# A list scheduler inside a kernel and its model of transfers: one path that all transfers pass in a line at one rate

## The chip, the cores and the metric

The kernel runs on one core of a Trainium2 chip. A core has five engines that run side by side, each with its own queue of instructions that it works off in order: TensorE (PE in the profile, with its weight loads as PEld), VectorE (DVE), ScalarE (ACT), GpSimd (POOL) and SyncE (SP). Transfers between the memories run on 16 DMA engines; here SP issues the plain ones and POOL the accumulating ones. The metric is the device time of one execution in microseconds (us); smaller is better.

## The reference

The input `x` is 32 images of 96 channels of 56 x 56 numbers. There are two layers. The first is an inverted-bottleneck convolution; the second works on the 3136 pixels of an image as tokens, mixes them by a Fourier transform, and ends with a two-layer network that rounds to 8-bit and 16-bit floats.

```python
# layer 0 (biases and batch norms are folded into the weights here)
h = relu(bn(einsum('oc,bchw->bohw', w1, x)))      # 96 -> 576 channels
h = relu(bn(dwconv3x3(h, wdw)))                   # 9 taps for each channel
x = x + bn(einsum('oc,bchw->bohw', w2, h))        # 576 -> 96
# layer 1, on tokens t of shape (32, 3136, 96)
h = relu(bn(layernorm(t) @ w1.T))                 # 96 -> 192
X = fft(h, axis=1)
xr = relu(X.real * rd - X.imag * id + rb)
xi = relu(X.imag * rd + X.real * id + ib)
t = t + bn(ifft(xr + 1j * xi).real @ w2.T)        # 192 -> 96
u = q8(layernorm(t))                              # rounded to e5m2
h = relu(q16(q16(u @ q8(W1).T) + q8(b1)))         # 96 -> 384
t = t + q16(q16(q8(h) @ q8(W2).T) + q8(b2))       # 384 -> 96
```

## The kernel before

The kernel cuts the work into some hundred *steps* for each image: a load, a group of matmuls, an eviction, one tap of the convolution, and so on. Each step names its engine, its estimated cost, the steps that it comes after, the buffers that it takes and gives back, and a rank. When the program is built, `Plan.emit` plays all steps through on a clock of its own: whenever an engine of the model is idle, it emits the ready step of the lowest rank whose buffers are free. **The order in which the steps are emitted is the order of the instructions in each engine's queue on the chip.** The clock of the model is never seen by the chip; the chip waits on semaphores, as the data demand. So a wrong estimate makes no wrong result, only an order in which an engine may stand before data that are not there yet.

```python
class Plan:
    LATE = {"PE": 0.3, "ACT": 0.18, "DVE": 0.15}   # from a step's end to those that wait for it
    ...
    def emit(self):
        ...
                    s.emit()                       # the real instructions are issued here, in this order
                    left -= 1
                    idle[engine] = False
                    cost = self.stretched(now, s.cost) if engine == "PE" else s.cost
                    ...
                    late = self.moved(now, s.late) if isinstance(s.late, tuple) else s.late
                    heapq.heappush(events, (now + cost, count, engine, None))   # the engine is free again
                    heapq.heappush(events, (now + cost + late, count + 1, None, s))  # followers may start
        ...
                if engine == "PE" and idle[engine] and work and now > FIRST and self.sparse(now):
                    self.filler()                  # a matmul that nobody reads, where TensorE would pause
```

A step that issues a transfer has a tuple as its `late`: the bytes, a rate and a fixed extra time. `moved` makes of it the time until the transfer's landing:

```python
    def moved(self, now, moves):
        size, rate, extra = moves
        start = now + 1.4
        end = start + size / rate
        self.moving = [m for m in self.moving if m[1] > start - 20]
        wait = sum(max(0.0, min(end, b) - max(start, a)) for a, b in self.moving)
        self.moving.append((start, start + 1.3 * size / rate))
        return end + wait + extra - now
...
    def read(n):
        return n * 4, 170e3, 1.5       # bytes, bytes per us, us
    def written(n):
        return n * 4, 170e3, 3.0
```

The convolution of layer 0 is where most transfers with an impatient reader lie. A *unit* is 128 channels of half an image, eight of them for an image. ScalarE makes the first tap and one or two further products, VectorE adds the other taps one by one, and an accumulating transfer of GpSimd adds the product to the sum; then ScalarE applies the relu in place, and TensorE reads the sum:

```python
        def add(to, dr):                           # line 678: acc += product, or product += product
            def f():
                ...
                nc.gpsimd.dma_start(out=..., in_=..., accum_op=ALU.add)
        def finish():                              # line 687
            nc.scalar.activation(acc[img, s, k], acc[img, s, k], AF.Relu)

        t = step("ACT", act(W, 2, 0.09), begin, e, ["acc"], rank=4 * n + OFF[1])        # line 643
        c = [step("ACT", act(W, 1, 0.09), product(0), e, ["product"], rank=4 * n + AT[0])]  # line 659
        ...
        for at, q in enumerate(rest):              # line 670, on DVE
            t = step("DVE", dve(W - 28, 0.16), tap(*q), [t] + c * last, [], ["hs"] * last, rank=...)
        if k in DOUBLE:                            # two units of four: product += product first
            c = [step("POOL", 1.0, add(0, -up), c, [], ["product"],
                      late=(W * 128 * 4, 200e3, 0.0), rank=4 * n + AT[1])]
        t = step("POOL", 1.0, add(None, 0), [t] + c, [], ["product"],
                 late=(W * 128 * 4, 200e3, 0.0), rank=4 * n + 3)
        ready[img, s, k] = step("ACT", act(W, 0, 0.09), finish, [t], rank=4 * n + OFF[3])
```

Other transfers: `xs` (half an image of input, 623,616 bytes), `tdr` (layer 0's result to memory, 602,112), `ydr` (first transform stage to memory, 602,112 in four pieces), `yb` (the same back in another order, 602,112 in two pieces), `wb` (702,464) and `wd` (357,504) with transform constants, `gdr` and `gd` (301,056 each, out and back), `tt` (301,056) and the output (301,056). Line 837 is the square root of a norm on ScalarE, line 853 the reciprocal on VectorE behind it; line 1491 is the filler.

Of the kernel before, what the change touches and what calls it, by code (L numbers as in the profile page):

```python
# [52 lines left out]
W = R * S  # L53
# [75 lines left out]
PACE = {"last": 3.023, "front": 0.4, "mid": 0.54, "back": 0.45}  # L129
CHAIN = 0.6  # L130

SPARSE = 0.75
FILLER = 0.23
FIRST = 15.0
# [2 lines left out]
AT = (3.0, 0.5)  # L137
# [6 lines left out]
class Step:  # L144
    def __init__(self, engine, cost, emit, after, take, give, late, rank, at):
        self.engine, self.cost, self.emit = engine, cost, emit
        self.take, self.give, self.late = take, give, late
        self.rank, self.at = rank, at
        self.left = len(after)
        self.next = []  # L150
        for a in after:
            a.next.append(self)


class Plan:
# [12 lines left out]
    def __init__(self, free):  # L168
        self.free = dict(free)
        self.steps = []  # L170
        self.now = self.pace = 0.0
        self.window, self.share, self.slow = 0, {}, False
        self.moving = []
        self.filler, self.recent = None, []

    def stretched(self, now, work):
# [18 lines left out]
    def sparse(self, now):  # L195

        self.recent = [r for r in self.recent if r[1] > now - self.WINDOW]
        return sum(b - max(a, now - self.WINDOW) for a, b in self.recent) < SPARSE * self.WINDOW

    def moved(self, now, moves):  # L200

        size, rate, extra = moves
        start = now + 1.4
        end = start + size / rate
        self.moving = [m for m in self.moving if m[1] > start - 20]
        wait = sum(max(0.0, min(end, b) - max(start, a)) for a, b in self.moving)
        self.moving.append((start, start + 1.3 * size / rate))
        return end + wait + extra - now

    def job(self, now, pace):  # L210

# [2 lines left out]
    def step(self, engine, cost, emit, after=(), take=(), give=(), late=None, rank=None):  # L214
        late = self.LATE.get(engine, 0.1) if late is None else late
        if rank is None:
            rank = self.now
            self.now += self.pace
        s = Step(engine, cost, emit, list(after), list(take), list(give), late, rank, len(self.steps))
        self.steps.append(s)  # L220
        return s
# [62 lines left out]
def tile_kernel(ctx: ExitStack, tc: tile.TileContext, d: dict, out: bass.AP):  # L284
# [12 lines left out]
    def psum():  # L297
        return psa.tile([128, 2, 512], F32, name="ps", tag="ps")
# [147 lines left out]
    for k in range(NK + 1):  # L446
# [5 lines left out]
            start=True,  # L452
# [101 lines left out]
    step = plan.step  # L554

    def pe(n, m, passes):
        return passes * max(0.855 * n, 0.88 * m) / 1000

    def act(n, columns=0, source=0.05):
        return source + 0.835 * n / 1000 + 0.093 * columns  # L560

    def dve(n, fixed=0.13):
        return fixed + n / 960

    def read(n):
        return n * 4, 170e3, 1.5

    def written(n):
        return n * 4, 170e3, 3.0

    bands_set = [step("DVE", 1.2, bands(j), rank=2.0 + j) for j in range(2)]
    sets = []
    for n, (f, count) in enumerate(((second, 7), (attention, 6), (mixer, 21), (ffn, 4))):
        t = step("SP", 0.55 * count, fetch, sets[-1:], late=(150e3, 170e3, 1.5), rank=-20.0 + n)
        sets.append(step("DVE", 3.0, f, sets[-1:] + [t], rank=14.0 + 4 * n))
    second_set, mixer_set, *mid_set = sets

# [22 lines left out]
    def unit(img, s, k):  # L600
        n = (2 * img + s) * NK + k
        o = R * s - base[s]
        up = 1 - 2 * s
        u = {}

        def weight(dr, dc):
            at = 3 * (dr + 1) + dc + 1
            return wdw[:, k, at : at + 1]

        def expand(h):  # L610
            def mm():
                if h == 0:
                    u["hs"] = w2.tile([128, XR, S], F32, name="hs", bufs=3)
                u[h] = psum()
                for j in range(2):
                    at = (2 * h + j) * QW
                    nc.tensor.matmul(  # L617
                        u[h][:, j, 0:QW],
                        lhsT=w1T[:, 128 * k : 128 * (k + 1)],
                        rhs=xs[img, s][0:C, at : at + QW],  # L620
                        start=True,
                        stop=True,
                    )

            def evict():
                flat = u["hs"].rearrange("p r c -> p (r c)")
                nc.scalar.activation(  # L627
                    flat[:, 2 * h * QW : 2 * (h + 1) * QW].rearrange("p (j w) -> p j w", j=2),
                    u[h][:, :, 0:QW],
                    AF.Relu,  # L630
                    bias=b1[:, k : k + 1],
                )

            after = [loaded[img, s]] if h == 0 else [u["first"]]
            e = u["first"] = step("PE", pe(QW, 128, 4), mm, after, ["ps"] + ["hs"] * (h == 0), rank=4 * n + OFF[0] + h)
            return step("ACT", act(2 * QW, 1), evict, [e], [], ["ps"], rank=4 * n + OFF[0] + h)

        e = [expand(0), expand(1)]

        def begin():  # L640

            acc[img, s, k] = w1.tile([128, R, S], F32, name="acc", bufs=7)
            nc.scalar.activation(  # L643
                acc[img, s, k],
                u["hs"][:, o + up : o + up + R, :],
                AF.Identity,
                scale=weight(up, 0),
                bias=bd[:, k : k + 1],
            )

        def span(dr, dc):

            return max(0, -(o + dr)), min(R, XR - o - dr), max(0, -dc), S - max(0, dc)

        def product(dr):
            def f():
                ra, rb, _, _ = span(dr, 0)
                u["p", dr] = w1.tile([128, R, S], F32, name="product", bufs=3)
                nc.scalar.activation(  # L659
                    u["p", dr][:, ra:rb, :], u["hs"][:, ra + o + dr : rb + o + dr, :], AF.Copy, scale=weight(dr, 0)  # L660
                )

            return f

        def tap(dr, dc):
            def f():
                ra, rb, ca, cb = span(dr, dc)
                src = u["hs"][:, ra + o + dr : rb + o + dr, ca + dc : cb + dc]
                dst = acc[img, s, k][:, ra:rb, ca:cb]
                nc.vector.scalar_tensor_tensor(dst, src, weight(dr, dc), dst, ALU.mult, ALU.add)  # L670

            return f

        def add(to, dr):
            def f():
                ra, rb, _, _ = span(dr, 0)
                t = acc[img, s, k] if to is None else u["p", to]
                nc.gpsimd.dma_start(  # L678
                    out=t[:, ra:rb, :].rearrange("p r c -> p (r c)"),
                    in_=u["p", dr][:, ra:rb, :].rearrange("p r c -> p (r c)"),  # L680
                    accum_op=ALU.add,
                )

            return f

        def finish():
            nc.scalar.activation(acc[img, s, k], acc[img, s, k], AF.Relu)  # L687

        t = step("ACT", act(W, 2, 0.09), begin, e, ["acc"], rank=4 * n + OFF[1])
        c = [step("ACT", act(W, 1, 0.09), product(0), e, ["product"], rank=4 * n + AT[0])]  # L690
        rest = [q for q in TAPS[1:] if q != (up, 0)]
        if k in DOUBLE:

            rest.remove((-up, 0))
            c.append(step("ACT", act(W, 1, 0.09), product(-up), e, ["product"], rank=4 * n + AT[1]))
        for at, q in enumerate(rest):
            last = q == rest[-1]
            t = step("DVE", dve(W - 28, 0.16), tap(*q), [t] + c * last, [], ["hs"] * last, rank=4 * n + OFF[2] + at * 3.5 / len(rest))
        if k in DOUBLE:
            c = [step("POOL", 1.0, add(0, -up), c, [], ["product"], late=(W * 128 * 4, 200e3, 0.0), rank=4 * n + AT[1])]  # L700
        t = step("POOL", 1.0, add(None, 0), [t] + c, [], ["product"], late=(W * 128 * 4, 200e3, 0.0), rank=4 * n + 3)
        ready[img, s, k] = step("ACT", act(W, 0, 0.09), finish, [t], rank=4 * n + OFF[3])

    def last_channels(img, s):
# [160 lines left out]
    def front(img, s):  # L865
# [80 lines left out]
        for i in range(G):  # L946
# [14 lines left out]
            if i in (3, 6):  # L961
                a = i - i % 4
                ev.append(step("ACT", act((i + 1 - a) * 2 * C), evict(a, i + 1), t, [], ["pw"]))
        taken[img, s] = t[0]
        sent[img, s] = step("SP", 0.1, keep, ev, late=written(2 * SK * G * C))
        t = norm(u, "a", RP, SK, ev, False, ["norma"], [])
        for j in range(2):
            mixer_in(img, s, j, u, t)

    def mixer_in(img, s, j, v, after):  # L970
# [87 lines left out]
        def send():  # L1058

            yv = ydr[img].rearrange("ri g (b p) h -> b (ri g) (p h)", b=2)  # L1060
            for b in range(2):
                for c in range(2):
# [4 lines left out]
                    )  # L1067

        sent[img, "y", h] = step("SP", 0.3, send, ends, [], ["ya"], late=written(SK * G * HA))


# [487 lines left out]
```

## Time and profile before

| what | value |
|---|---|
| time, median of 3 executions (lowest to highest) | 4589.91 us (4589.24 to 4595.37) |
| span of the profiled execution | 4584.2 us, 88412 instructions |
| TensorE clock granted, mean | 0.988 of full speed |
| accumulating transfers, GpSimd's queue | 304.64 MB, 34.4% of the DMA engines' time |
| plain transfers, SyncE's queue | 479.15 MB, 36.2% of the DMA engines' time |
| chain that ended last, by engine | PE 48%, ACT 22%, DVE 16%, DMA 8%, issue 4% |

The profile is one execution on the chip. A *group* is all instructions of one source line on one engine; of each the profile gives the busy time, the mean duration and the engine's idle time just before them, with what ended it. "ACT acc L687 <- DMA acc<-product" reads: ScalarE stood idle before instructions of line 687, which write `acc`, until a transfer from `product` to `acc` had landed. The busy share of an engine is taken over the whole span; in a full pipeline the idle time of the fullest engine is the most that another order can win.

### The profile page before, as it was taken

What the parts mean: (1) busy time and instruction counts of PE and PEld (TensorE: products, weight loads), DVE (VectorE), ACT (ScalarE), POOL (GpSimd) and SP (SyncE); (2) the same over time, 40 slices, a digit from 0 to 9 for tenths busy, and PEclk for the clock granted to TensorE, in tenths of its full rate; (3) what the DMA queues carried; (4) which work ended last, traced back from release to release, by engine and by line L of the source; (5) the groups of instructions that cost most, each with busy time, mean ns of one, the idle gap of its engine ahead of it and who ended that gap; (6) DMA issues with size and microseconds to landing.
All of it is one profiled execution on the core that took longest, in us unless ns stands there. A gap on an engine that the chain in (4) does not pass through costs nothing.

```text
span 4584.2 us, 88412 instructions
## 1 busy us (share of the span) xinstructions
PE 4405.4 (96%) x35128; PEld 3296.1 (72%) x35128; DVE 4330.6 (94%) x7053; ACT 4114.5 (90%) x5390; POOL 340.7 (7%) x403
## 2 busy tenths in 40 slices
PE   8989999999999999999999999999999999999998
PEld 5667776777777777777777777777777777777777
DVE  8998999999999999999999999999999999999967
ACT  5677999999999999999999999999999999999965
POOL 1000000000000000000000000000000000000000
PEclk9999999999999999999999999999999999999999
DMA  4666777767767777767777767777767777767663
GB/s 104 135 155 157 190 171 176 187 162 185 181 163 188 174 179 185 184 166 191 173 176 185 183 163 188 174 176 183 187 162 188 174 174 190 179 165 191 168 170 107
DMA packets 390993, 789.44 MB, mean 172 GB/s; under 512 B 135696, under 2 KB 236628, under 8 KB 390580
## 3 DMA queue, kind: packets, MB, share of 16 engines
q1 hardware_dynamic: 335028, 479.15, 36.2%
q0 software_dynamic: 55488, 304.64, 34.4%
q8 instruction: 276, 4.52, 0.4%
q14 instruction: 137, 1.12, 0.1%
q10 hardware_dynamic: 64, 0.01, 0.0%
HBM read 286.38 MB, written 192.68 MB: 105 GB/s over the span
## 4 chain that ended last, share of the span: by engine, by line
PE 48%; ACT 22%; DVE 16%; DMA 8%; issue 4%; POOLq 0%; ACTq 0%; POOL 0%; SPq 0%; DVEq 0%
PE pw L883 11%; DVE acc L670 10%; PE ps L617 9%; DMA acc<-product 7%; PE ps L1005 4%; PE ps L1123 4%; PE ps L755 3%; PE ps L1036 3%; ACT product L659 3%; ACT hs L627 2%; ACT acc L687 2%; ACT acc L643 2%; PE ps L1329 2%; ACT h L1410 2%; ACT h L1395 2%
## 5 line engine op out<-in xcount | busy, mean ns | idle before, releaser
L670 DVE SCALAR_TENSOR_TENSOR acc<-hs,wdw,acc 128x1540 f32<-128x1540 f32 (+2 forms) x1664 | 2970.3, 1792 | 26.6 <-ACT acc L643 20.8
L617 PE MATMUL ps<-xs,w1T 96*128 96x406 f32 x2048 | 819.8, 523 | 24.6 <-ACT h L1395 16.7
L883 PEld LDWEIGHTS pw<-w2T,acc 128*112 128x112 f32 x7168 | 754.3, 178 | 62.1 <-issue 36.4
L883 PE MATMUL pw<-w2T,acc 128*112 128x96 f32 x7168 | 790.8, 264 | 4.5 <-ACT acc L687 4.5
L659 ACT ACTIVATE product<-hs,wdw 128x1568 f32<-128x1568 f32 (+1 forms) x384 | 613.8, 1599 | 21.6 <-DMA product<-product 20.9
L617 PEld LDWEIGHTS ps<-xs,w1T 96*128 96x128 f32 x2048 | 368.2, 194 | 261.7 <-issue 174.0
L627 ACT ACTIVATE hs<-ps,b 128x812 f32<-128x812 f32 x512 | 481.5, 941 | 51.2 <-PE ps L617 46.8
L687 ACT ACTIVATE acc<-acc 128x1568 f32<-128x1568 f32 x256 | 387.5, 1514 | 90.9 <-DMA acc<-product 85.1
L678 POOL DMA_DIRECT2D acc<-product x256 | 222.7, 870 | 3193.9 <-DVE mf L859 781.6
L643 ACT ACTIVATE acc<-hs,bd,wdw 128x1568 f32<-128x1568 f32 x256 | 437.0, 1707 | 0.3
L755 PE MATMUL ps<-hl,band 128*64 128x385 f32 (+3 forms) x3072 | 416.1, 495 | 0.3 <-ACT hs L627 0.3
L1005 PE MATMUL ps<-watt,xnT 97*120 97x192 f32 x1792 | 345.3, 337 | 60.9 <-DVE V L1152 59.6
L1005 PEld LDWEIGHTS ps<-watt,xnT 97*120 97x120 f32 x1792 | 299.0, 187 | 125.3 <-DVE V L1152 65.6
L1123 PEld LDWEIGHTS ps<-wb,yb 112*128 112x128 f32 x3528 | 297.3, 164 | 66.5 <-issue 20.9
L1395 ACT ACTIVATE h<-ps 128x784 f16<-128x784 f32 x384 | 319.6, 835 | 25.8 <-PE ps L1383 22.0
L1350 ACT ACTIVATE u<-tt,mf,rf 112x96 fp8e5<-112x96 f32 x812 | 312.3, 460 | 16.6 <-DVE mf L859 16.5
L1123 PE MATMUL ps<-wb,yb 112*128 112x112 f32 x3528 | 321.8, 271 | 4.4 <-ACT hs L627 2.6
L1410 ACT ACTIVATE h<-h 128x784 fp8e5<-128x784 f16 x348 | 301.9, 867 | 14.9 <-DVE h L1401 14.8
L755 PEld LDWEIGHTS ps<-hl,band 128*64 128x64 f32 (+1 forms) x3072 | 151.9, 134 | 198.9 <-issue 164.2
L1152 DVE SCALAR_TENSOR_TENSOR sb<-ps,cw,V 128x784 f32<-128x784 f32 x192 | 197.0, 1026 | 31.1 <-ACT V L1136 25.4
L1018 ACT ACTIVATE z<-ps 120x768 f32<-120x768 f32 (+1 forms) x256 | 182.3, 725 | 44.9 <-PE ps L1005 44.9
L1036 PE MATMUL ps<-z,wa 56*64 56x384 f32 (+1 forms) x2048 | 217.5, 496 | 0.3
(171 smaller groups left out, 6663.3 us busy)
## 6 DMA issues: line engine op xcount, KB each, us to landing
acc<-product POOLq DMA_DIRECT2D x256, 784.0 KB, 8.0
product<-product POOLq DMA_DIRECT2D x128, 756.0 KB, 10.1
yb<-ydr SPq DMA_DIRECT2D x252, 294.0 KB
wd<-in_wd_dram SPq DMA_DIRECT2D x128, 349.1 KB
wb<-in_wb_dram SPq DMA_DIRECT2D x63, 686.0 KB
ydr<-ya SPq DMA_DIRECT2D x256, 168.0 KB
xs<-in_x_dram SPq DMA_DIRECT2D x64, 609.0 KB
tdr<-xt SPq DMA_DIRECT2D x64, 588.0 KB
```

The source lines that it names most:

```text
L617: nc.tensor.matmul(u[h][:, j, 0:QW], lhsT=w1T[:, 128 * k : 128 * (k + 1)], rhs=xs[img, s][0:C, at : at + QW], start=True, stop=True,)
L627: nc.scalar.activation(flat[:, 2 * h * QW : 2 * (h + 1) * QW].rearrange("p (j w) -> p j w", j=2), u[h][:, :, 0:QW], AF.Relu, bias=b1[:, k ...
L643: nc.scalar.activation(acc[img, s, k], u["hs"][:, o + up : o + up + R, :], AF.Identity, scale=weight(up, 0), bias=bd[:, k : k + 1],)
L659: nc.scalar.activation(u["p", dr][:, ra:rb, :], u["hs"][:, ra + o + dr : rb + o + dr, :], AF.Copy, scale=weight(dr, 0))
L670: nc.vector.scalar_tensor_tensor(dst, src, weight(dr, dc), dst, ALU.mult, ALU.add)
L687: nc.scalar.activation(acc[img, s, k], acc[img, s, k], AF.Relu)
L755: nc.tensor.matmul(pv[:, :, ca:cb], lhsT=band[rows, j, dc + 1, 64 * o : 64 * o + 64], rhs=H[rows, q : q + 7, ca + dc : cb + dc], skip_grou ...
L883: nc.tensor.matmul(u["pw"][0:SK, t, n % 4, 0:C], lhsT=src[rows, (G * t + n) * SK : (G * t + n + 1) * SK], rhs=rhs, skip_group_check=True, **k,
L1005: nc.tensor.matmul(pv[0:PK, q - a, 0:HA], lhsT=xnT[:, q, 0:PK], rhs=watt, start=True, stop=True,)
L1123: nc.tensor.matmul(o, lhsT=lhsT, rhs=u["wb"][:, G * s + q, :], start=True, stop=True)
L1395: nc.scalar.activation(u["h", c].rearrange("p (j w) -> p j w", j=2), u["H", c][:, :, 0:n], AF.Copy)
L1410: nc.scalar.activation(u["h8"][:, c, :], u["h", c], AF.Copy, saturate=False)
```

## The change

Only the scheduler's model of transfers changes. Before, every transfer had a rate of its kind (170 GB/s, or 200 GB/s for accumulations) and was lengthened by its overlap with the intervals of the others, each drawn out by 1.3; what those others had been lengthened by themselves was not counted. After, all transfers share one path: each starts on it when the one before has left it, and no sooner than 1.0 us after its issue; it passes at 225 GB/s, and lands 0.5 us after it has left the path, or 1.3 us after if it is one of GpSimd's accumulations. The purpose is an estimate that keeps account of a backlog, so that the order of the steps fits the time at which data really come. Costs, ranks, buffers and every emitted instruction's form are as before.

```diff
+RATE = 225e3
+HARD = 0.5
+SOFT = 1.3
...
-        self.moving = []
+        self.moving = 0.0
...
     def moved(self, now, moves):
 
-        size, rate, extra = moves
-        start = now + 1.4
-        end = start + size / rate
-        self.moving = [m for m in self.moving if m[1] > start - 20]
-        wait = sum(max(0.0, min(end, b) - max(start, a)) for a, b in self.moving)
-        self.moving.append((start, start + 1.3 * size / rate))
-        return end + wait + extra - now
+        size, extra = moves
+        self.moving = max(self.moving, now + 1.0) + size / RATE
+        return self.moving + extra - now
...
     def read(n):
-        return n * 4, 170e3, 1.5
+        return n * 4, HARD
 
     def written(n):
-        return n * 4, 170e3, 3.0
+        return n * 4, HARD
...
-        t = step("SP", 0.55 * count, fetch, sets[-1:], late=(150e3, 170e3, 1.5), rank=-20.0 + n)
+        t = step("SP", 0.55 * count, fetch, sets[-1:], late=(150e3, HARD), rank=-20.0 + n)
...
-            c = [step("POOL", 1.0, add(0, -up), c, [], ["product"], late=(W * 128 * 4, 200e3, 0.0), rank=4 * n + AT[1])]
-        t = step("POOL", 1.0, add(None, 0), [t] + c, [], ["product"], late=(W * 128 * 4, 200e3, 0.0), rank=4 * n + 3)
+            c = [step("POOL", 1.0, add(0, -up), c, [], ["product"], late=(W * 128 * 4, SOFT), rank=4 * n + AT[1])]
+        t = step("POOL", 1.0, add(None, 0), [t] + c, [], ["product"], late=(W * 128 * 4, SOFT), rank=4 * n + 3)
```

## The prediction

> **What bounds the kernel now.** I read the page's busy times first, then the waits of each engine, then three whole image periods, and last the instructions around the one wait on a transfer that recurs in every image.
>
> ```profile
> PE 4405.4 (96%) x35128; PEld 3296.1 (72%) x35128; DVE 4330.6 (94%) x7053; ACT 4114.5 (90%) x5390; POOL 340.7 (7%) x403
> ...
> DMA packets 390993, 789.44 MB, mean 172 GB/s; under 512 B 135696, under 2 KB 236628, under 8 KB 390580
> ...
> acc<-product POOLq DMA_DIRECT2D x256, 784.0 KB, 8.0
> product<-product POOLq DMA_DIRECT2D x128, 756.0 KB, 10.1
> ```
>
> Three engines are nearly full. VectorE (DVE) is the floor: its 4330.6 us cannot shrink, because the change adds and removes no instruction of it. TensorE's 4405.4 us contain 207.1 us of filler matmuls (the group of line 1491, 1382 of them), which only fill its pauses, so its own work is about 4198 us. The whole span leaves DVE idle for 4584.2 - 4330.6 = 254 us. The stretch from 4350 us to the end alone has 234 us with 83.95 + 48.46 + 35.24 = 168 us of DVE work, so 66 us of that idle time is the last image draining, and 23 us more lie in the first 230 us. Some 165 us remain in the 4120 us between, and only these can be won or enlarged by another order.
>
> The next view is of busy times in three image periods (start:end, length, then each engine's busy us with its count). An image's period is the distance between two equal points of its work.
>
> ```profile
> 1055.50:1195.50 140.00, 136.15 (x1078) 101.33 (x1076) 133.20 (x215) 130.11 (x174) 10.45 (x12) 0.98 0.72 176
> 1612.90:1749.70 136.80, 133.17 (x1078) 99.00 (x1076) 133.06 (x215) 129.80 (x174) 10.46 (x12) 1.00 0.74 181
> 2161.30:2299.00 137.70, 134.62 (x1078) 99.81 (x1076) 133.20 (x215) 130.18 (x174) 10.46 (x12) 0.99 0.74 178
> ```
>
> DVE (third busy figure) has 133.1 to 133.2 us in each; only its pauses differ: 6.8, 3.7 and 4.5 us. From the 530.3 us to the 4259.7 us mark are 27 such periods, 138.1 us on average.
>
> Who waits, from 1000 to 4350 us, in ACT's and DVE's own lists (total us, times, longest):
>
> ```profile
> ACT acc L687 <- DMA acc<-product: 48.6, 24, 3.2
> ACT al L784 <- PE ps L755: 32.4, 25, 1.3
> ...
> DVE rf L853 <- ACT sdf L837: 42.4, 47, 2.5
> DVE sb L1152 <- ACT V L1136: 19.9, 50, 0.4
> ```
>
> ACT's longest wait is on a transfer, the accumulation of a product, just once per image. No wait of TensorE names a transfer. Here is that wait in one image, in the timeline (start, us, engine, line; idle before it in brackets):
>
> ```profile
> 2154.31 0.28 SPq L1301 DMA_DIRECT2D wd<-in_wd_dram  x1
> ...
> 2155.40 0.86 POOL L678 DMA_DIRECT2D acc<-product  x1 [14.74 <-DVE da L834]
> ...
> 2156.51 0.86 POOL L678 DMA_DIRECT2D product<-product  x1 [0.25 <-ACT product L659]
> ...
> 2164.24 1.51 ACT L687 ACTIVATE acc<-acc 128x1568 f32<-128x1568 f32 x1 [1.22 <-DMA acc<-product]
> ...
> 2165.66 0.19 ACT L837 ACTIVATE sdf<-wf 112x7 f32<-112x7 f32 x1
> ...
> 2165.89 0.20 DVE L853 RECIPROCAL rf<-sdf 112x7 f32<-112x7 f32 x1 [0.55 <-ACT sdf L837]
> ```
>
> The scheduler put the relu (L687) on ACT's queue 1.22 us before its sum had landed; the square root (L837) stands behind it, and DVE's reciprocal waits 0.55 us for that. In the 140.0 us period the same three places show 1.99 us on ACT and 1.31 us on DVE. So one forecast error of the scheduler becomes idle time of the floor engine.
>
> **What the Trainium skill says.** "Perfetto Trace Analysis", section "Tensor Engine Instruction (MATMUL, LD_WEIGHTS)", states that ACT and DVE are strict FIFO; the timeline agrees: work behind the relu stands still with it. "DMA: Bandwidth & Descriptors", section "Issuing engines are not separate DMA queues", says transfers of all issuers run on the same 16 DMA engines and interleave. The trace agrees on the shared path: an accumulation takes between 5.6 and 17.4 us to land, whatever else moves. Its section "Queues, rings and completion order" says that each DMA engine goes round the queues packet by packet. So a later transfer can delay an earlier one of another queue, which a strict line denies. The trace agrees here too: the product accumulation issued at 2190.09 had nothing ahead of it but landed after 10.1 us, as three more transfers were issued in the next microsecond.
>
> **The change, part by part.** Its direct work on the chip is zero: same matmuls, vector operations and transfers. What differs is the list scheduler's guess of when a transfer lands, so where the steps that need it stand in the queues. The number of fillers may move too.
>
> The constants. A lone accumulation (802,816 B) was forecast at 1.4 + 802816/200000 = 5.41 us, and becomes 1.0 + 802816/225000 + 1.3 = 5.87; the shortest landing in the trace is 5.6. A lone 602,112 B load goes from 1.4 + 3.54 + 1.5 = 6.44 to 1.0 + 2.68 + 0.5 = 4.18, and a store of that size from 7.94 to 4.18. The rate is plausible: the four largest queues' shares (36.2, 34.4, 0.4, 0.1%) sum to 71.1% at a mean of 172 GB/s, thus 172/0.711 = 242 GB/s when all are busy.
>
> The line. Before, the waiting time was the overlap with others' undelayed intervals, so a backlog was forgotten. I put the real issue times up to 2156.51 through both formulas (the scheduler's own issue times differ somewhat). New: the line starts at 2136.16, 1.0 after a 702,464 B load. Issued by 2155.40 are that, 602,112, 802,816, two of 301,056, two of 602,112, 623,616, 602,112, 357,504 and the accumulation's 802,816 B: 6,299,776 B, or 28.0 us at 225 kB/us. It leaves the line at 2164.16 and lands at 2165.46, 10.1 us after issue. The trace has 8.8 us (2164.22). The product behind it: 2164.16 + 3.57 + 1.3 = 2169.03; the trace has 2168.7. Old: start 2156.80, end 2160.81; the only overlap is 1.64 us with the wd load's interval (2155.71 to 2158.44), hence 2162.45, 7.05 us: 1.8 us too early. The product's old forecast is 9.96 us against 12.2. So at the wait that recurs, the new forecast is late enough for other ready work, the L1410 and L627 steps that stood behind the relu, to go first.
>
> The same calculation for all accumulations between 300 and 4300 us gives these errors (trace less forecast): into acc, 232 of them, old mean 0.32 with a standard deviation of 1.56 us, new 0.22 with 0.95; between products, 116, old mean 2.56, new 1.32. The new model is better here. Loads get shorter forecasts, from 7.8 to 6.0 us on average; their truth I cannot see in these records.
>
> The worth. ACT's waits on both kinds of accumulation are 85.1 + 20.9 = 106 us in the whole run, but ACT is not the floor. What reaches DVE: of the 42.4 us of DVE's rf wait, about 0.41 us in each of 24 periods is another visit that no transfer causes (9.8 us); 32.6 us over 24 periods, 1.36 us each, are the relu's stall. Over 31 periods this is 42 us. Not all is kept: a DVE pause removed here partly returns at the next handover, and a new order brings pauses of its own. I give back 17 us, a choice about which I know only that good and bad periods in this trace differ by 3 us with the same work. Sum: -42 + 17 = -25 us, which makes 4590 - 25 = 4565 us; the mean period would be about 137.3 us.
>
> **Rivals.** First, nothing: list order follows ranks more than readiness, so most forecasts never decide anything. For it: TensorE never waits for a transfer, so shorter load forecasts change little. Against it: the recurrent wait, which is decided by a forecast. It would give 4580 to 4600 us.
>
> Second, a wait that takes its place: optimistic loads (-1.8 us) and stores (4.18 instead of 7.94 us alone) pull mixer and second-layer steps forward, until TensorE or the in-order SP queue stands before data not yet there. SP already waits 199.7 us, 45 times, before a gd load for the gdr stores; on the traced issue times the backlog raises that store's forecast from 7.6 to 8.8 us, which speaks against it. So does the lack of any wait of TensorE now. It would make 4600 to 4650 us.
>
> Third, the new order settles in a different cycle all through. The trace has periods from 135.6 to 140.0 us. At 136 everywhere the gain is 2.1 x 31 = 65 us (4525), at 139.5 the loss 1.4 x 31 = 43 us (4633). The ranks and start offsets were chosen with the old model, which speaks for some harm.
>
> **Range and chances.** The centre is 4565. The lower end takes almost the good cycle, 4525; the upper end takes the second rival in a mild form, 4612. A gain above 2% means under 4498 us, 92 us of the 165 that exist: 0.04. A loss above 2% means over 4682 us, three more idle us in every image: 0.03. The rest, 0.93, lies within 2%.
>
> **What would show it.** Right: ACT's wait L687 for the accumulation falls from 85.1 us to under 45, DVE's rf wait from 55.4 to under 35, DVE's busy sum stays at 4330 within 5, the mean period is near 137.3 us. Wrong: new waits of TensorE on gd, yb or xs, a higher SP wait for gdr, or waits L659 on the product buffers above 40 us, because forecasts hold that buffer longer; or ACT's wait gone with DVE as idle as before, which would mean the stall was covered elsewhere.

## The result, and the profile after

The new kernel takes 4482.92 us (median of 4; 4477.31 to 4484.93) against 4589.57 us for the one before (median of 4; 4583.93 to 4595.37). The ratio is 0.9766, 95% interval 0.9749 to 0.9783: 2.3% faster, well below the predicted 4525 to 4612 us.

First the page of the kernel after: busy times, the mean DMA rate, and the median time to landing of the accumulations.

```profile
PE 4370.5 (98%) x35032; PEld 3258.5 (73%) x35032; DVE 4306.3 (96%) x7053; ACT 4097.3 (92%) x5390; POOL 338.9 (8%) x403
...
DMA packets 390993, 789.44 MB, mean 176 GB/s; under 512 B 135696, under 2 KB 236628, under 8 KB 390580
...
acc<-product POOLq DMA_DIRECT2D x256, 784.0 KB, 8.7
product<-product POOLq DMA_DIRECT2D x128, 756.0 KB, 11.2
```

The work is the same: 7053 instructions on VectorE, 5390 on ScalarE, the same packets and bytes. Only TensorE has 96 fewer filler matmuls. The transfers did not get faster: by the medians, accumulations land a little *later* than before (8.7 and 11.2 us, formerly 8.0 and 10.1), and the mean landing into acc is the same, 8.6 us. The time came from the order.

Three image periods of the kernel after (start:end, length, then busy us with counts for PE, PEld, DVE, ACT and POOL, granted clock, DMA share, GB/s):

```profile
1034.90:1169.40 134.50, 133.25 (x1072) 98.20 (x1070) 132.12 (x215) 129.43 (x174) 10.38 (x12) 1.00 0.76 183
1572.80:1707.30 134.50, 133.13 (x1072) 98.41 (x1070) 132.22 (x215) 129.18 (x173) 10.38 (x12) 1.00 0.75 183
2111.30:2245.80 134.50, 133.12 (x1072) 98.42 (x1070) 132.21 (x215) 129.19 (x173) 10.39 (x12) 1.00 0.75 183
```

Before, the three shown in the prediction took 136.8 to 140.0 us. Now most take 134.5 us, and the granted clock is full in all three. Between the 495.4 and 4130.6 us marks, the mean of 27 periods is 134.6 us.

Waits of ScalarE and VectorE from 1000 to 4350 us, kernel after:

```profile
ACT al L784 <- PE ps L755: 45.2, 48, 1.0
...
ACT acc L687 <- DMA acc<-product: 2.3, 7, 0.7
...
DVE h L1401 <- ACT h L1395: 66.9, 78, 6.4
...
DVE rf L853 <- ACT sdf L837: 0.9, 2, 0.6
```

ScalarE's wait for a sum went from 48.6 to 2.3 us in this stretch, and VectorE's wait behind the square root from 42.4 to 0.9. What is left on VectorE is another handover (h, 13.7 us before, 66.9 now), in 78 pieces of 0.9 us in the mean. The same place of the image in the timeline after (start, us, instruction; no bracket means no idle time before it):

```profile
2238.92 0.28 SPq L1301 DMA_DIRECT2D wd<-in_wd_dram  x1
2239.75 0.86 POOL L678 DMA_DIRECT2D acc<-product  x1 [14.96 <-ACT pj L1235]
2241.11 0.86 POOL L678 DMA_DIRECT2D product<-product  x1 [0.49 <-ACT product L659]
...
2248.67 0.19 ACT L837 ACTIVATE sdf<-wf 112x7 f32<-112x7 f32 x1
2249.59 1.50 ACT L687 ACTIVATE acc<-acc 128x1568 f32<-128x1568 f32 x1
2249.77 0.19 DVE L853 RECIPROCAL rf<-sdf 112x7 f32<-112x7 f32 x1
```

The pair of accumulations is still there. But the square root (L837) now stands *ahead* of the relu (L687), and the relu starts 1.5 us after its sum has landed (issue to landing was 8.3 us), without a pause before it.

**Two clocks.** The list scheduler's own clock, read when the program is built, is useful here. It ended at 4488.7 us for the kernel before and at 4474.0 us after, and in both it has the same period, 135.1 us, from the seventh image on. So the scheduler believed both orders almost equal. The chip ran 101 us behind that clock before, and 9 us after. By this count, 15 of the 107 us gained are a shorter plan, and about 92 are a plan that the chip can keep. The 15 us come from the last two images: up to the thirtieth image the new plan mostly runs 1 to 4 us *later* than the old one.

Which relu was too early can be read from the traces. For each of an image's eight units, this is how long after the landing of its sum the relu started, mean of images 8 to 29, worked out from the landings and ScalarE's records:

```
unit (half, number)    (0,0) (0,1) (0,2) (0,3) (1,0) (1,1) (1,2) (1,3)
before, us              2.72  1.55  0.67  2.17  1.10  2.24  0.02  2.30
after, us               0.30  1.94  1.98  1.99  4.54  1.22  1.46  3.27
```

Before, unit (1,2) alone started at the very landing, with ScalarE idle for 2.04 us in front of it. Its forecast in the plan was 6.8 us, its landing 9.6 in the mean.

### The profile page after: what moved, and what is told of

It reads as the page before. It is cut to its first block, busy times and chain, and to the rows that moved or that the text cites. A ratio compares the mean times of both kernels' runs of the same rounds, so it can differ in the third digit from the quotient of the medians.

```text
span 4475.5 us, 88222 instructions
## 1 busy us (share of the span) xinstructions
PE 4370.5 (98%) x35032; PEld 3258.5 (73%) x35032; DVE 4306.3 (96%) x7053; ACT 4097.3 (92%) x5390; POOL 338.9 (8%) x403
## 4 chain that ended last, share of the span: by engine, by line
PE 43%; DVE 33%; ACT 13%; issue 5%; DMA 4%; SPq 0%; DVEq 0%; POOL 0%; POOLq 0%; ACTq 0%
DVE acc L670 22%; PE pw L883 10%; PE ps L617 7%; PE ps L755 4%; PE ps L1005 4%; PE ps L1123 3%; PE ps L1036 3%; DMA acc<-product 3%; DVE V L1152 2%; DVE sb L1152 2%; PE ps L1428 2%; ACT h L1395 2%; ACT acc L687 1%; PE ps L1329 1%; ACT product L659 1%
## 5 line engine op out<-in xcount | busy, mean ns | idle before, releaser
L617 PE MATMUL ps<-xs,w1T 96*128 96x406 f32 x2048 | 808.6, 518 | 25.0 <-ACT al L784 12.6
L617 PEld LDWEIGHTS ps<-xs,w1T 96*128 96x128 f32 x2048 | 356.3, 190 | 288.7 <-issue 167.0
L687 ACT ACTIVATE acc<-acc 128x1568 f32<-128x1568 f32 x256 | 387.4, 1513 | 31.9 <-DMA acc<-product 26.0
L1401 DVE TENSOR_SCALAR h<-h,b1q 128x784 f16<-128x784 f16 x384 | 162.5, 423 | 84.6 <-ACT h L1395 84.4
L1329 PE MATMUL ps<-gd,wd 114*112 114x96 f32 x1792 | 199.5, 263 | 8.6 <-DMA gd<-gdr 3.6
## 6 DMA issues: line engine op xcount, KB each, us to landing
product<-product POOLq DMA_DIRECT2D x128, 756.0 KB, 11.2
```

The lines of the kernel that those rows point to most:

```text
L617: nc.tensor.matmul(u[h][:, j, 0:QW], lhsT=w1T[:, 128 * k : 128 * (k + 1)], rhs=xs[img, s][0:C, at : at + QW], start=True, stop=True,)
```

## The experiments

Each kernel was timed beside the kernel before on the same chip (whose medians were 4591.24, 4591.64 and 4592.14 us there). Three theories stood at the start. A: one misplaced relu, with everything behind it, is most of the loss. B: the new order is a lucky cycle as a whole. C: the shorter forecasts of the loads count.

### The relu alone, moved later

In the old order, with the old forecasts, only this relu is held back:

```diff
-                    s.emit()
+                    if getattr(s, "hold", 0):
+                        held = [s.emit, s.hold]          # emitted after s.hold further ACT steps
+                    else:
+                        s.emit()
+                        if held and engine == "ACT": ... # count down, then held[0]()
...
+        ready[img, s, k].hold = 3 * ((s, k) == (1, 2))
```

> The old forecasts and the old order, but the one relu per image that stood too early (second half image, third unit) is issued three ScalarE places later. Theory A (this one misplaced relu, with the pauses and clock drops behind it, is most of what before lost on the chip against the scheduler's own clock of 4489 us): 4490 to 4530 us, ScalarE's wait for the accumulation under 25 us, and almost no half-clock windows after 800 us. Theory B (the new order wins as a whole, by a lucky cycle; the relu is a small part, as predicted): 4550 to 4575. Theory C (the loads' shorter forecasts are what counts): no change, 4585.

Measured: 4501.66 us (4498.78 to 4505.07), ratio 0.9813 (0.9794 to 0.9832). Waits of ScalarE, VectorE and TensorE from 1000 to 4300 us (lines are moved by 10 or 11 by the edit: 697 is the relu, 864 the reciprocal, 848 the square root, 1016 is 1005):

```profile
ACT acc L697 <- DMA acc<-product: 5.0, 11, 0.9
...
DVE sb L1163 <- ACT V L1147: 19.5, 49, 0.5
...
DVE rf L864 <- ACT sdf L848: 6.8, 23, 1.3
...
PE ps L1016 <- DVE V L1163: 2.1, 2, 1.2
```

In the kernel before, the same stretch also has the three waits below. The first two are gone with the relu moved, and the third falls from 50.5 to 2.1 us:

```profile
DVE h L1401 <- ACT h L1395: 13.7, 22, 1.2
DVE acc L670 <- ACT acc L643: 12.7, 24, 1.3
...
PE ps L1005 <- DVE V L1152: 50.5, 24, 2.1
```

One instruction per image in another place, and 90 us are gone. The period falls to 135.0 us in the mean, often 134.6, close to the new kernel's. Between the two profiled executions (4584.2 and 4498.0 us) VectorE's idle time fell by 74 us and its recorded busy time by 12. What remains to the new kernel, 19 us, is near the 15 us by which the two plans differ; that it is the same time is not shown. Theory A holds for the kernel before.

### The converse: one relu of the new order, moved earlier

The new order is kept; the relu of unit (0,0) goes three ScalarE places ahead, which the trace of the new kernel puts 2.2 us before the landing.

```diff
-                    s.emit()
+                    order.append((engine, s.emit, getattr(s, "early", 0)))   # emitted at the end, in this order
...
+                order.insert(at, order.pop(i))        # at: three ACT entries ahead
...
+        ready[img, s, k].early = 3 * ((s, k) == (0, 0))
```

> The converse: the new order, but the relu of the first unit of each image is issued three ScalarE places earlier; in the new kernel's trace that place lies 2.2 us before its sum has landed. Everything else stands as in the new order. If one such relu is the cause: 4540 to 4590 us, ScalarE waiting some 2 us per image for that accumulation. If before's loss was special to its order: 4483 to 4510.

Measured: 4603.18 us, ratio to the kernel before 1.0025 (1.0016 to 1.0035). That is 120 us above the new kernel: the whole gain and more. Waits of ScalarE, VectorE and TensorE from 1000 to 4300 us (697 is the relu, 1406, 1412 and 1134 are lines 1395, 1401 and 1123 moved by the edit):

```profile
ACT acc L697 <- DMA acc<-product: 50.0, 24, 3.2
...
DVE h L1412 <- ACT h L1406: 92.4, 94, 3.0
DVE rf L864 <- ACT sdf L848: 28.8, 23, 1.3
...
PE ps L1134 <- ACT h L1406: 23.9, 23, 2.1
```

The stall is as long as the old one (2.14 us per image on ScalarE) and stands elsewhere in the image; it costs more, a little over the size expected. Part of the excess may be the clock: the profiled execution, the slowest of twenty, has 92 us of half-clock windows from 800 to 4300 us, against 58 in the kernel before. So the loss belongs to no special place of the old order. Theory B, as a lucky cycle of which the relu is a small part, falls with both runs.

### Where the 90 us are lost: fillers in front of TensorE's pause

Behind the old stall TensorE paused too: 50.5 us in 24 pauses from 1000 to 4350 us before line 1005, waiting for VectorE. Here six fillers per image are issued there:

```diff
             def f():
+                if h == 0 and i == 1:
+                    for _ in range(6):
+                        plan.filler()
                 u["p", i] = psum()
```

> The old forecasts and the old order, with six more filler matmuls per image (on TensorE, in front of the second projection of the first quarter of an image), where before TensorE paused 2.1 us per image behind the misplaced relu. Separates the pause itself from the half-clock window that follows it. If the clock drops are most of the chain's cost: 4520 to 4560 us and hardly a half-clock window after 800 us. If the relu's delay itself is: 4575 to 4595.

Measured: 4568.37 us (4557.37 to 4572.25), ratio 0.9940 (0.9919 to 0.9960). Waits of TensorE and ScalarE from 1000 to 4350 us (1008 and 1155 are lines 1005 and 1152 moved by the edit):

```profile
PE ps L1008 <- DVE V L1155: 19.4, 24, 1.6
...
ACT acc L687 <- DMA acc<-product: 45.0, 26, 2.8
```

The relu waits as before. But the record of the granted clock has no half-clock window from 800 to 4300 us any more; the kernel before has 12, together 58.0 us, the new kernel and the one with the relu moved have none. All twelve start within 2 us of the end of one of these pauses. At half speed, 58.0 us are an estimated 29 us of lost matmul work at most, and the median fell by 23 (18 to 37 by the interval of the ratio). So about 23 of the 90 us go back to TensorE at half speed after its pause. The rest, some 67 us, I put down to the pauses themselves by subtraction; no run takes it apart. The median lies between the two ranges expected and meets neither.

### Half the change at a time

Two kernels keep both models, and take the landing of a kind from one or the other; all transfers pass through both, so that each model sees the whole traffic.

```diff
+        self.moving = max(self.moving, now + 1.0) + size / RATE
+        line = self.moving + (SOFT if rate == 200e3 else HARD) - now
         ...                                              # the old formula
-        return end + wait + extra - now
+        return line if (rate == 200e3) == ADDS else end + wait + extra - now
```

`ADDS = True`, new forecasts for accumulations only:

> Accumulations get the line's forecast, loads and stores keep the old one. The scheduler's own clock ends at 4496 us. Theory A: the chip follows that clock, 4495 to 4525, with ScalarE waiting under 35 us for accumulations. Theory B: anywhere from 4500 to 4600. Theory C: 4560 to 4600.

Measured: 4604.97 us, ratio 1.0032 (1.0021 to 1.0043). `ADDS = False`, new forecasts for loads and stores only:

> The reverse: loads and stores get the line's forecast, accumulations keep the old one. The scheduler's own clock ends at 4500 us. Theory A: the chip falls behind that clock by some 60 to 100 us, 4560 to 4600, with waits of ScalarE for accumulations above 60 us. Theory B: 4500 to 4600. Theory C: 4500 to 4520.

Measured: 4645.97 us (4637.68 to 4650.49), ratio 1.0123 (1.0104 to 1.0142).

A's expectation of the first kernel failed clearly, and the second is slower than all three theories had it; ScalarE waited there for 37.4 us from 1000 to 4300 us, not for over 60. ScalarE's waits from 1000 to 4350 us of the kernel with new accumulation forecasts (694 is the relu):

```profile
ACT acc L694 <- DMA acc<-product: 69.1, 32, 4.6
```

The plan alternates between two kinds of image there. In the one, unit (0,0) was forecast at 5.9 us, an empty line, and landed after 10.1; unit (1,0) was forecast at 8.8 and landed after 12.0. Their relus waited 30.5 and 29.1 us in 11 images each. In the other kernel (1,2) was forecast at 6.4 us in every other image and landed after 11.3, and VectorE met a wait that no other version has (1341 is line 1334 moved by the edit):

```profile
DVE tt L1341 <- DMA tt<-tdr: 21.0, 11, 2.9
```

So neither half carries the gain, and theory C falls. The two halves fail in different ways, as the traced issue times show when they are put into the line's formula. For (1,2) of the second kernel the line gives about 12 us: there the old formula was wrong. For (0,0) of the first kernel it gives 5.9 us again, in ten of the eleven images: there the line itself was wrong. By its reckoning nothing stood ahead, but four transfers of SyncE, 1.26 MB, were issued within 2.1 us *behind* this accumulation, here in one image (685 is line 678; the second of the two yb is issued at 1213.24):

```profile
1211.14 0.86 POOL L685 DMA_DIRECT2D acc<-product  x1 [14.18 <-ACT h L1417]
1211.39 0.27 SPq L1308 DMA_DIRECT2D wd<-in_wd_dram  x1
1211.71 0.32 SPq L1311 DMA_DIRECT2D gd<-gdr  x1
1212.88 7.41 SPq L1101 DMA_DIRECT2D yb<-ydr  x2
...
1221.08 1.51 ACT L694 ACTIVATE acc<-acc 128x1568 f32<-128x1568 f32 x1 [2.36 <-DMA acc<-product]
```

This is the weakness that the prediction named: a later transfer delays an earlier one of another queue. In the new kernel the same four transfers are issued 3.4 to 1.5 us *ahead* of this accumulation, where the line counts them: forecast 8.7 us, landing 9.6.

### Right on average, without a line

```diff
-        self.moving = max(self.moving, now + 1.0) + size / RATE
-        return self.moving + extra - now
+        return extra          # 5.5 plain, 8.4 into acc, 10.5 between products
```

> No line at all: every transfer gets a constant, close to the mean that the new model gives its kind (accumulation into acc 8.4 us, between products 10.5, loads and stores 5.5). The scheduler's own clock ends at 4493 us. Theory A: right on average is not enough where a backlog makes landings 9.6 to 13 us; the chip falls behind the clock by 30 to 80 us, 4520 to 4570. If the line is not needed and only the mean level counts: 4490 to 4515.

Measured: 4748.73 us (4740.32 to 4755.90), ratio 1.0349 (1.0328 to 1.0369): worse than either expectation, the slowest of all, though its forecasts miss accumulations into acc by only 0.4 us on average (those between products land 0.9 us earlier than forecast). Single ones are off by much: unit (0,2) lands after 12.7 us instead of 8.4, (1,3) after 6.6. But ScalarE waits for sums for only 45.3 us from 1000 to 4300 us, about as in the kernel before. What grew is TensorE's wait for VectorE before line 1005, in the same stretch 94.7 us after 50.5 (1004 and 1151 are lines 1005 and 1152 here), and its half-clock windows, 184 us from 800 to 4300 us. Which misplaced step costs most is open.

```profile
PE ps L1004 <- DVE V L1151: 94.7, 46, 2.4
```

```diff
-late=(W * 128 * 4, 200e3, 0.0)
+late=(W * 128 * 4, 200e3, 1.5)
```

This one adds 1.5 us to each accumulation in the old model.

> The old model with 1.5 us more for each accumulation, which corrects its mean and not its pattern. The scheduler's own clock ends at 4580 us. If the mean level of the forecasts were the fault: 4490 to 4530. If single landings have to be right: no gain over before, 4560 to 4640.

Measured: 4622.37 us (4621.48 to 4631.92), ratio 1.0066 (1.0047 to 1.0085). This does not settle the question of the mean level: the plan is 91 us longer, the chip falls behind it by 43 us and not by 101, and into acc the forecasts are now 1.3 us too late on average where they were 1.0 us too early. It shows only that this much more for every accumulation is no cure.

### The line's rate, and constants beside it

`RATE = 250e3`:

> The new model with the line's rate at 250 GB/s in place of 225. The scheduler's own clock ends at 4473 us, 1 us earlier than the new kernel's. If the forecasts' truth decides: forecasts become too short by 1 us and more behind a backlog, so the chip falls behind the clock by 20 to 80 us, 4490 to 4555, with ScalarE waiting for accumulations. If the form of the model is enough whatever its rate: 4475 to 4490.

Measured: 4522.31 us (4516.87 to 4529.87), ratio 0.9844 (0.9825 to 0.9863), 50 us behind its clock, as expected in size. But ScalarE waits for accumulations for only 9.7 us from 1000 to 4300 us, so the loss does not lie in the relus' waits; that part of the expectation failed. Between the profiled executions of this kernel and the new one, VectorE's recorded busy time is 20 us longer and its idle time 25; why is open.

`RATE = 200e3`:

> The new model with the line's rate at 200 GB/s. The scheduler's own clock ends at 4584 us. If the forecasts' truth decides: now too long, so the plan itself is slow, and the chip holds it or beats it by a little, 4530 to 4590, with almost no wait of ScalarE for accumulations. If late forecasts cost nothing: below 4500.

Measured: 4651.12 us (4644.79 to 4657.53), ratio 1.0128 (1.0104 to 1.0152). I had thought the chip would hold a pessimistic plan or beat it; it fell 67 us behind. Late forecasts cost twice here: the plan itself is longer, and its periods are uneven (135 to 143 us on its own clock), with single landings again off (the errors spread by 2.1 us).

Three kernels with other constants near the new ones, chosen for an early end of the scheduler's clock: 230 GB/s with 1.8 us after the line for accumulations; 235 GB/s with 1.0 and 1.8 us; 240 GB/s with 0.5 and 2.3 us.

> The new model with 230 GB/s and 1.8 us after the line for accumulations, the scheduler's own clock ending at 4470 us (new kernel 4474), periods even from the tenth image on. If forecasts stay true enough: 4475 to 4490. If the new kernel's place is a narrow one: 4500 to 4540.

> The new model with 235 GB/s, 1.0 us after the line for plain transfers and 1.8 for accumulations, the scheduler's own clock ending at 4472 us, periods even from the sixth image on. If forecasts stay true enough: 4475 to 4490. If the new kernel's place is a narrow one: 4500 to 4540.

> The new model with 240 GB/s and 2.3 us after the line for accumulations, the scheduler's own clock ending at 4477 us, periods even from the seventh image on. If forecasts stay true enough: 4480 to 4495. If the new kernel's place is a narrow one: 4500 to 4540.

Measured: 4477.21 us (ratio 0.9747, 0.9720 to 0.9774), 4474.16 us (0.9740, 0.9708 to 0.9772), 4490.17 us (0.9775, 0.9748 to 0.9802). The second is 9 us below the new kernel's median, but the intervals of the two ratios overlap. The first and third lie in the range expected, the second 0.8 us under it. The gain is no single lucky point: four sets of constants keep it.

All runs in one table. The spread is the standard deviation of landing less forecast for accumulations into acc, images 8 to 29.

| kernel | scheduler's clock, us | chip, us | chip behind clock | spread, us |
|---|---|---|---|---|
| before | 4489 | 4590 | 101 | 1.05 |
| after | 4474 | 4483 | 9 | 0.75 |
| relu later (old order) | 4489 | 4502 | 13 | 1.19 |
| relu earlier (new order) | 4474 | 4603 | 129 | 1.39 |
| line for accumulations only | 4496 | 4605 | 109 | 1.46 |
| line for loads and stores only | 4500 | 4646 | 146 | 1.92 |
| fillers in the pause (old order) | 4489 | 4568 | 80 | 1.04 |
| fixed forecasts | 4493 | 4749 | 256 | 2.20 |
| old, accumulations + 1.5 us | 4580 | 4622 | 43 | 1.63 |
| rate 250 | 4473 | 4522 | 50 | 0.92 |
| rate 200 | 4584 | 4651 | 67 | 2.11 |
| 230; 0.5, 1.8 | 4470 | 4477 | 7 | 0.70 |
| 235; 1.0, 1.8 | 4472 | 4474 | 2 | 0.87 |
| 240; 0.5, 2.3 | 4477 | 4490 | 13 | 0.89 |

Among those whose clock ends at 4489 to 4500 a larger spread mostly goes with a larger gap. The two relu runs show that it isn't the spread as such: their plans and forecasts are those of their parents, and one place in ScalarE's queue decides. So the cause of most of the gain, that no relu stands before its sum any more, is shown; that truer forecasts made the good order is argued, for the line for accumulations alone did not make one.

## Why the prediction was wrong, step by step

**What bounds the kernel.** Nearly right. VectorE is the floor, and most of the gain is its idle time: of the 109 us between the two profiled executions, 84. "Cannot shrink" was wrong: its recorded busy time fell from 4330.6 to 4306.3 us with the same instructions, and these are the other 24, so idle time was not all that another order could win.

**The recurrent wait.** Right. It named the relu, the square root and reciprocal behind it, and moving that relu alone brought most of the gain.

**The forecasts.** Right in direction: errors into acc fell from a spread of 1.05 us in the old plan to 0.75 in the new one. My hand-worked 10.1 us did not come; in the new order the pair has other traffic ahead, was forecast at 7.8 and landed after 8.4 in the mean.

**The worth.** This step failed: "32.6 us over 24 periods, 1.36 us each, are the relu's stall. Over 31 periods this is 42 us". The mechanism was right, the term was mis-sized. I sized it by the first VectorE wait behind the relu. The run that moves the relu puts the term at 90 us, about 2.9 us over each of 31 periods. It exceeds even ScalarE's own stall of 2.04 us, since the delay went on: to further VectorE waits (74 us of its idle time went, not 42), to TensorE's pause of 2.1 us before line 1005, and to half-clock windows after that (23 us of the 90). The waits all stood in the lists that I had read, and I counted one.

**The part given back.** "I give back 17 us" was wrong in sign: the new plan is 15 us shorter on its own clock, though only at its end. With 90 + 15 in place of 42 - 17, the sum is 4590 - 105 = 4485 us.

**The rivals.** The third went the right way, "the new order settles in a different cycle all through", but I took the trace's best periods, 135.6 to 136 us, as its floor. VectorE's 133.2 us of work were the floor to set, and the chip came within 1.5 us of it; hence also a range that ended too high. The second did not come: no wait of TensorE on a transfer above 4 us in total, and SP's wait for gdr fell from 199.7 to 173.6 us.

**What would show it.** ScalarE's wait fell to 26.0 us in the whole run (said: under 45), VectorE's rf wait to 2.9 (under 35); the period is 134.6 and not 137.3. VectorE's busy sum left the range of 4330 within 5.

## What to carry to other kernels

Where a static order is laid down by a model, look at what runs behind the model's own clock on the chip, and find the one instruction per period that stands before its data; moving it alone is a cheap test of the whole theory. Price such a stall by all engines that pass it on, not by the first wait behind it: here 2.0 us on ScalarE cost 2.9 us per image. A forecast matters where it decides such a place, and there it has to be right for this one transfer, with what is issued ahead of it and just behind it: the fixed forecasts, right on average into acc, gave the slowest kernel of all.

## What the runs showed of the hardware that I had not expected

A crude line describes the shared DMA engines fairly well in the orders that it made itself: start 1.0 us after issue, 225 to 240 GB/s, 1.3 to 2.3 us to the landing of an accumulation; landings into acc then came within 0.7 to 0.9 us (standard deviation) of the forecast. It is no law of all orders. With the traced issue times in both formulas (the pieces of a step taken as one), the line at 225 GB/s misses landings into acc with a standard deviation of 0.8 to 1.5 us over the fourteen kernels, the old formula with 0.9 to 2.2; in the new kernel's own traffic the two are close, 0.95 and 1.05.

An accumulation lands later when much is issued right behind it. Of those into acc that the line finds clear at the traced issue times (all fourteen kernels, images 8 to 29), 346 had under 0.3 MB issued within 3 us behind them and landed after 6.0 us in the mean; 60 had 1.2 MB or more and landed after 8.3.

In the kernel before, 12 of the 25 pauses of TensorE before line 1005 from 800 to 4300 us, nearly all of them 2.1 us long, had a half-clock window of 3.4 or 6.8 us start within 2 us of their end; most of the others were just as long and had none, so the length alone does not decide. Six fillers in that pause removed all these windows, and the run was 23 us shorter.

VectorE's recorded busy time differs with the order: 4330.6 us before, 4318.8 with the relu moved, 4306.3 after, for the same 7053 instructions. Worked out from all starts and durations, neighbours in the queue overlap by 517 us in all before and by 572 us after, while the durations' sum rose by 30 us. With the relu moved the overlap is 521 us, hardly more than before, and the durations' sum 9 us lower. So no one reason fits both; it stays open.
